# First image of two chained attention layers: the half blocks from the sixth on are loaded in 128-byte runs and turned by VectorE

## The chip, the cores and the metric

One core of a Trainium2 chip runs the whole program. The metric is the device time of one execution in microseconds (us), the median of the runs. A core has five engines that work at the same time and wait for one another by semaphores: TensorE (PE, and PEld for its weight loads), VectorE (DVE), ScalarE (ACT), GpSimd (POOL) and SyncE (SP). Each takes its own instructions in the order in which they stand in the program. SP and POOL here mostly start DMA transfers.

## What is computed

Two self-attention layers over four images of 64x64 pixels with 256 channels, that is 4096 tokens of 256 float32 values per image:

```python
# layer 0, per image: x is (4096, 256)
q, k, v = x @ Wq + bq, x @ Wk + bk, x @ Wv + bv        # 32, 32 and 256 wide
x = gamma * (softmax(q @ k.T) @ v) + x
# layer 1
g, f, v = x @ Wg + bg, x @ Wf + bf, x @ Wh + bh        # 32, 32 and 128 wide
x = x + (softmax(g @ f.T) @ v) @ Wo + bo
```

## The kernel before

The kernel goes through image `b`, layer `l`, block of queries `j` and, innermost, step `i` over groups of keys. In layer 0 a block has 256 queries and a step takes 512 keys, so there are eight steps. `Step.scores` makes the scores `st` (L532) and their exponentials `high` and `p` (L542, L544); `cut_low` and `cut_both` split the rounding off into `low` and `d` (L555, L560); `products_first` multiplies the parts with the parts of v (L580).

Before an image can be attended to, its tokens have to be projected. This is done by half blocks of 256 tokens, `h` from 0 to 15 (`NH`), and `project_units(b, l, h)` returns three pieces of work:

- `transpose_unit` makes `xT`, the tokens turned so that channels lie on the partitions, and its two parts `xh` (L405, ScalarE) and `xl` (L406, VectorE), in the list `x_parts`.
- `qk_unit` makes the projections q and k in the bank `psqk` (L422), collects them in `qk` and splits them into `qk_parts` (L439 to L442), writes these to DRAM (`qk_dram`, L446, on SP) and, in the first image, loads k straight from them by four transfers on POOL (`load_k`, L493).
- `v_unit` makes v in the bank `psv` (L464) and its three parts `v0h`, `v0l`, `v0d` (L480 to L483).

There are two ways to turn a half block. For image 0, layer 0, the tokens are loaded as they lie (`load_first`, tiles `x_nat`, L300), turned by TensorE into a PSUM bank `psx` (L389) and copied out by ScalarE (L390). `LEAD` = 5 halves are loaded at the start; from then on the transpose of half h starts the load of half h+5. In all other cases `load_squares` fetches a half with eight transfers of 32 channels each (L280), whose runs are 32 values, 128 bytes, in such a way that squares of 32x32 values lie where VectorE's transpose of such squares (L392) turns them into `xT`.

The banks `psx`, `psqk` and `psv` come from a pool of two, `ps_side`. In SBUF, image 0 also uses buffers that layer 1 needs only later: the tag `v1` (10 buffers, `V1`) holds `x_nat`, and the tag `v1_parts` (6 buffers, `LEAD_BUFS`) holds `xT`, both parts and `qk_parts` of the odd halves. The even halves have buffers of their own (`xT`, `squares`, `qk_parts`).

The first six halves of image 0 are projected ahead of all steps (L685 to L689). The other ten go two by two into the first five steps: at the head of step i the transposes of halves 2(i+3) and 2(i+3)+1 are written (`early`, L761 to L763), and their `qk_unit` and `v_unit` follow behind part of the products (L789 to L790). Later images are projected during layer 1 of the image before.

The text gives the order in which work is named; a scheduler then sets the order in which the instructions of each engine stand, from its own estimate of when the inputs are there. That order is fixed when the kernel runs.

## Time and profile before

| | |
|---|---|
| three runs | 3155.88 us median, 3155.57 to 3157.44 |
| the profiled execution | 3156.87 us, its span 3155.1 us |
| busy: PE, DVE, ACT, POOL | 3117.6, 2689.3, 2138.5, 898.7 us |
| granted TensorE clock | 0.998 of full speed |
| projection of image 0, layer 0 (first to last `xT` copy of L390) | from 5.6 to 79.0 us |
| L389 transposes on TensorE | 64 instructions, 0.299 us each |
| L390 copies on ScalarE | 16, 0.584 us each |
| `x_nat` loads on SP | 32 of 128 KB |

The profile is of one execution. Its times are microseconds from the start of the span; TensorE's ends are modelled, and its matmuls overlap, so a busy TensorE isn't one at its peak. A line of a timeline gives the start, the busy time, engine, line and operation, the tiles written and read with their shapes, and in brackets for how long the engine had been idle before, and what ended that.

### The profile page before, as it was taken

Reading aid. Unit: us, or ns where it says so; the run is one execution under the profiler, and the core shown is the slowest. Engines: PE = TensorE matmul, PEld = TensorE weight load, DVE = VectorE, ACT = ScalarE, POOL = GpSimd, SP = SyncE. Lnnn points to the kernel's source line nnn. Section 1 sums busy time; section 2 is a strip of 40 time slices with the busy share of each in tenths; the row PEclk is TensorE's granted clock in tenths of the full one; section 3 lists DMA queues with packets and bytes.
Section 4 is the critical chain, followed back from the end, with each engine's and each line's share of the span. In section 5 each row is a group of like instructions: output and inputs, shape, how many; then the busy total and the mean of one; then the engine's idle time right before and its main releaser. Section 6 shows DMA issues by size and latency. Waiting matters only on the chain.

```text
span 3155.1 us, 54090 instructions
## 1 busy us (share of the span) xinstructions
PE 3117.6 (99%) x19908; PEld 2674.3 (85%) x19908; DVE 2689.3 (85%) x3237; ACT 2138.5 (68%) x2835; POOL 898.7 (28%) x1108
## 2 busy tenths in 40 slices
PE   8999999999999999999999999999999999999997
PEld 7999998666799999866689999976668999996664
DVE  7888888888888888988888888888888888888876
ACT  7666666777666666777766666677776666666664
POOL 5222224222422222422242222332223222233221
PEclk9999999999999999999999999999999999999999
DMA  4121114555512121455541112255554111125454
GB/s 122 40 53 47 47 49 104 108 105 107 102 43 51 43 51 47 113 101 112 107 94 45 50 44 53 51 117 105 106 113 80 48 46 46 49 66 105 97 96 73
DMA packets 391392, 239.49 MB, mean 76 GB/s; under 512 B 266672, under 2 KB 355248, under 8 KB 391120
## 3 DMA queue, kind: packets, MB, share of 16 engines
q0 software_dynamic: 68160, 134.86, 22.0%
q1 hardware_dynamic: 322048, 100.76, 13.3%
q8 instruction: 161, 2.64, 0.4%
q14 instruction: 111, 0.91, 0.1%
q10 hardware_dynamic: 912, 0.33, 0.0%
HBM read 82.58 MB, written 67.11 MB: 47 GB/s over the span
## 4 chain that ended last, share of the span: by engine, by line
PE 91%; DVE 3%; issue 2%; DMA 2%; ACT 1%; POOL 0%; SPq 0%; DVEq 0%; ACTq 0%; POOLq 0%
PE acc L580 23%; PE acc_pair L580 23%; PE acc L598 23%; PE st L532 14%; PE psv L464 4%; PE psqk L422 2%; PE pso L665 2%; DVE low L555 1%; DMA squares<-in_x 1%; DVE d L560 1%; ACT p L544 1%; DVE p_sum L573 1%; DMA p_sum_moved<-p 0%; PE pso L666 0%; DMA squares<-x_dram 0%
## 5 line engine op out<-in xcount | busy, mean ns | idle before, releaser
L542 ACT ACTIVATE high<-st,down 128x1024 fp32r<-128x1024 f32 x704 | 785.8, 1116 | 707.2 <-PE st L532 419.5
L544 ACT ACTIVATE p<-st 128x1024 f32<-128x1024 f32 x1024 | 1042.2, 1021 | 167.5 <-PE st L532 145.8
L560 DVE SCALAR_TENSOR_TENSOR d<-low,high 128x1024 fp32r<-128x1024 f32 x704 | 870.5, 1237 | 227.7 <-PE acc_pair L580 222.3
L555 DVE TENSOR_TENSOR low<-p,high 128x1024 fp32r<-128x1024 f32 x704 | 938.5, 1333 | 142.7 <-ACT p L544 141.7
L532 PE MATMUL st<-q,k 128*128 128x256 f32 (+1 forms) x3072 | 703.7, 337 | 2.8 <-issue 1.3
L598 PE MATMUL acc<-p,v 128*128 128x512 f32 x1280 | 611.0, 597 | 0.0
L532 PEld LDWEIGHTS st<-q,k 128*128 128x128 f32 x3072 | 470.7, 189 | 102.9 <-issue 41.3
L637 POOL TENSOR_TENSOR x_res<-x,bo 128x256 f32<-128x256 f32 x128 | 213.9, 1671 | 879.5 <-DVE x L626 879.4
L598 PEld LDWEIGHTS acc<-p,v 128*128 128x128 f32 x1280 | 233.2, 189 | 161.8 <-issue 143.4
L573 DVE TENSOR_TENSOR p_sum<-p_sum,p 128x1024 f32<-128x1024 f32 x288 | 352.6, 1224 | 10.4 <-ACT p L544 6.8
L580 PE MATMUL acc<-v0h,high 128*128 128x258 f32 x2048 | 342.4, 284 | 1.2 <-ACT high L542 1.2
L580 PE MATMUL acc<-v0d,d 128*128 128x258 f32 x2048 | 339.3, 287 | 2.4 <-DVE d L560 2.0
L580 PE MATMUL acc<-v0l,low 128*128 128x258 f32 x2048 | 331.5, 283 | 0.6 <-DVE low L555 0.5
L580 PE MATMUL acc_pair<-v0l,low 128*128 128x258 f32 x2048 | 331.1, 283 | 0.0
L580 PE MATMUL acc_pair<-v0h,high 128*128 128x258 f32 x2048 | 329.6, 283 | 0.0
L580 PE MATMUL acc_pair<-v0d,d 128*128 128x258 f32 x2048 | 329.0, 283 | 0.0
L580 PEld LDWEIGHTS acc<-v0h,high 128*128 128x128 f32 x2048 | 287.2, 189 | 3.1 <-issue 1.4
L580 PEld LDWEIGHTS acc<-v0d,d 128*128 128x128 f32 x2048 | 280.9, 189 | 5.4 <-DVE d L560 4.7
L580 PEld LDWEIGHTS acc<-v0l,low 128*128 128x128 f32 x2048 | 281.7, 190 | 1.8 <-DVE low L555 1.3
L580 PEld LDWEIGHTS acc_pair<-v0h,high 128*128 128x128 f32 x2048 | 282.4, 189 | 0.0
L580 PEld LDWEIGHTS acc_pair<-v0l,low 128*128 128x128 f32 x2048 | 281.8, 189 | 0.0
L580 PEld LDWEIGHTS acc_pair<-v0d,d 128*128 128x128 f32 x2048 | 281.8, 189 | 0.0
(108 smaller groups left out, 3326.6 us busy)
## 6 DMA issues: line engine op xcount, KB each, us to landing
p_sum_moved<-p POOLq DMA_DIRECT2D x160, 512.0 KB, 4.8
x_res<-in_x SPq DMA_DIRECT2D x128, 128.0 KB, 2.1
qk_dram<-qk_parts SPq DMA_DIRECT2D x128, 128.0 KB, 1.8
x_dram<-x SPq DMA_DIRECT2D x128, 128.0 KB, 1.7
out<-x_res SPq DMA_DIRECT2D x128, 128.0 KB, 1.7
squares<-x_dram SPq DMA_DIRECT2D x512, 32.0 KB, 2.0
out<-y POOLq DMA_DIRECT2D x128, 128.0 KB, 3.2
q<-qk_dram POOLq DMA_DIRECT2D x252, 64.0 KB, 2.2
```

The source lines that it names most:

```text
L422: nc.tensor.matmul(ps, wqk[l][:, c, :], x_parts[key][n][:, c, :], start=(c == n == 0), stop=(c == NCC - 1 and n == 1),)
L464: nc.tensor.matmul(ps[:, t, :], xT[key][:, c, t * P : (t + 1) * P], wv[l][:, c, :], start=(c == 0), stop=(c == NCC - 1),)
L532: nc.tensor.matmul(st[:, g, :], k_t[b, l, kt // NT][:, kt % NT * P : (kt % NT + 1) * P], q_t[b, l, j * n // QB][:, q0 : q0 + n], start=Tru ...
L542: nc.scalar.activation(self.high, s_flat, AF.Exp, bias=down)
L544: nc.scalar.activation(self.p, s_flat, AF.Exp)
L555: nc.vector.tensor_sub(self.low, self.p, self.high.bitcast(F32))
L560: nc.vector.scalar_tensor_tensor(self.d, self.low.bitcast(F32), -UP, self.high.bitcast(F32), ALU.mult, ALU.add)
L573: nc.vector.tensor_add(p_sum, p_sum, self.p)
L580: nc.tensor.matmul(acc[2 * s + which][:, :W], p[:, g * QB0 + s * P : g * QB0 + (s + 1) * P], v0[self.i][v][:, g, :], start=self.first and ...
L598: nc.tensor.matmul(acc[which], v_part[:, g, :], p[:, g * QB : (g + 1) * QB], start=first and g == 0, stop=last and g == G[1] - 1,)
L637: nc.gpsimd.tensor_add(x_old[s], x_new[s], bo_sb)
L665: nc.tensor.matmul(ps[:, :C], part, wo_sb, start=True, stop=True)
```

## The change

From half 5 on, image 0 takes the second way too. `load_first` stops after the first five halves. The transpose of half h, from h = 3 on, starts the load of half h+2 with `load_squares`, into buffers of the tag `v1_parts`; and for h of 5 and above `transpose_unit` takes the branch with VectorE's transpose. Nothing else is edited: the split into parts, the projections and the attention are as they were, and so are the later images.

```diff
+    LEAD_BUFS = sum(split[1])
 
     def load_squares(key, tokens):
 
-        t = work.tile([P, NCC, QB0], F32, tag="squares", bufs=2, name="squares_" + "_".join(map(str, key)))
+        first = key[:2] == (0, 0)
+        t = (data if first else work).tile(
+            [P, NCC, QB0],
+            F32,
+            tag="v1_parts" if first else "squares",
+            bufs=LEAD_BUFS if first else 2,
+            name="squares_" + "_".join(map(str, key)),
+        )
         for c in range(NCC):
             for a in range(P // S):
                 ch = c * P + a * S
...
-    LEAD_BUFS = sum(split[1])
     LEAD = V1 // NS
 
     def load_first(h):
-        if h < NH:
+        if h < LEAD:
             x_nat[h] = []
...
-            if b == l == 0:
+            if b == l == 0 and h < LEAD:
                 ps = side_psum(f"psx_{h}").rearrange("p (c n) -> p c n", c=NCC)
...
             nc.scalar.copy(x_parts[key][0], xT[key])
             nc.vector.tensor_sub(x_parts[key][1], xT[key], x_parts[key][0].bitcast(F32))
-            if b == l == 0:
-                load_first(h + LEAD)
+            if b == l == 0 and h + 2 >= LEAD:
+                load_half(b, h + 2)
```

## The prediction

> **What bounds the kernel now.** I read the page first (engine totals, then the chain that ended last), then busy time by stretches over the first 100 us, then VectorE's and ScalarE's timelines there, then the line of the VectorE transposes.

> ```profile
> PE 3117.6 (99%) x19908; PEld 2674.3 (85%) x19908; DVE 2689.3 (85%) x3237; ACT 2138.5 (68%) x2835; POOL 898.7 (28%) x1108
> ...
> PE 91%; DVE 3%; issue 2%; DMA 2%; ACT 1%; POOL 0%; SPq 0%; DVEq 0%; ACTq 0%; POOLq 0%
> ```

> Over the span TensorE sets the time. But the change acts only while the first image is projected, so only that stretch may be asked. Five stretches, one for each step that projects two half blocks:

> ```profile
> 34.45:45.90 11.45, 11.42 (x76) 10.27 (x75) 9.53 (x14) 9.50 (x21) 4.96 (x11) 1.00 0.42 105
> 45.90:56.97 11.07, 9.70 (x61) 8.17 (x58) 8.56 (x15) 7.89 (x16) 5.06 (x11) 1.00 0.40 101
> 56.97:65.91 8.94, 8.16 (x51) 7.21 (x52) 6.27 (x11) 6.71 (x13) 2.69 (x6) 1.00 0.33 83
> 65.91:75.82 9.91, 9.56 (x61) 8.43 (x60) 7.83 (x13) 7.99 (x17) 3.88 (x8) 1.00 0.24 55
> 75.82:85.56 9.74, 9.37 (x62) 8.31 (x60) 7.72 (x12) 7.83 (x17) 3.88 (x8) 1.00 0.24 55
> ```

> After the length come PE, PEld, DVE, ACT and POOL. TensorE is nearly full here too, but VectorE and ScalarE work 8 of 10 us each, so this stage is a relay among three engines. VectorE's part of one step:

> ```profile
> 75.70 1.23 DVE L555 TENSOR_TENSOR low<-p,high 128x1024 fp32r<-128x1024 f32 x1 [0.77 <-ACT p L544]
> 76.95 0.42 DVE L442 TENSOR_TENSOR qk_parts<-qk,qk_parts 64x256 fp32r<-64x256 f32 x1
> 77.40 1.23 DVE L560 SCALAR_TENSOR_TENSOR d<-low,high 128x1024 fp32r<-128x1024 f32 x1
> 78.55 0.68 DVE L482 SCALAR_TENSOR_TENSOR v0d<-v0h,psv 128x512 fp32r<-128x512 f32 x1
> 79.14 0.68 DVE L406 TENSOR_TENSOR xl<-xT,xh 128x512 fp32r<-128x512 f32 x1
> 79.75 0.68 DVE L483 SCALAR_TENSOR_TENSOR v0l<-v0d,v0h 128x512 fp32r<-128x512 f32 x1
> 80.35 0.68 DVE L406 TENSOR_TENSOR xl<-xT,xh 128x512 fp32r<-128x512 f32 x1
> ```

> The two `xl` stand 1.2 us apart: the next two halves are turned and split early, side by side, while the last half's `v0d`, `v0l` and the step's `d` fill VectorE. The pitch is that of `psv` of the odd halves, 64.07, 73.99, 83.91: 9.92 us.

> ```profile
> L392 DVE STREAM_TRANSPOSE xT<-squares x112: 685/704/715, 113.6 to 2864.8; 128x512 f32<-128x512 f32 x112
> ```

> ```profile
> squares<-in_x SPq DMA_DIRECT2D x384, 32.0 KB, 2.5
> x_nat<-in_x SPq DMA_DIRECT2D x32, 128.0 KB, 3.0
> ```

> So the new operations have prices here, from the later images: 0.704 us for a transpose, 2.5 us to land.

> [...] `v0d` at 78.55 was ready at 77.19, when the reading of the accumulator ended, and waited behind `d`. [...] 1.25 us from `low` (75.70) to `qk_parts`, which writes partitions 64 to 127, but 1.15 from `d` (77.40) to `v0d`. [...]

> **The change, part by part.** Halves 5 to 15 change.

> Removed: 44 TensorE transposes (four advance the chain of waits by 0.44 us: 4.8 us), 11 ScalarE copies (0.586 each, 6.4 us), 22 loads on SP (0.41 each by 37.03, 9 us).

> Added: 11 VectorE transposes (7.7 us) and 88 loads on SP. Their issue has a median of 0.45 us: 40 us. Per step SP issues 16x0.45+2x0.34 = 7.9 us, which fits either pitch.

> Buffers: the allocator's placement puts even halves' `squares` where an `xl`, `xT` or `xh` had been, and odd ones from 11 on where the previous odd `squares` stood. That load waits for its transpose. SP in one step: after the last `qk_dram` eight loads for half h+2, eight for h+3, then `qk_dram` of h and h+1. The second eight start at 7.2 us into the step (below), take 3.6 to issue (5.1 at the worst group's 5.08 for eight) and 2.5 to land, so are there by 15; their transpose comes at 20. `qk_dram` of h is up to 3 us later than it could be; its buffer is next written about 7 us after that has landed. Hidden. The transpose in turn waits for its eight loads, and all of VectorE's queue stands behind it, ScalarE's `xh` too; by these times that wait is over before the queue gets there.

> What isn't hidden is the order. In the built program the VectorE order of one steady step (h even) is: T(h), xl(h), qk(h), v0d(h), v0l(h), T(h+1), low, xl(h+1), qk_parts(h), d, qk(h+1), v0d(h+1), v0l(h+1), qk_parts(h+1), T(h+2). T is the transpose. Each T stands behind the whole projection of the half before it, so the halves run one after the other. I walk through it with rows of before, T(h) starting at 0.

> Even half. T ends at 0.70; `xh` on ScalarE (0.62) ends at 1.35; TensorE starts `psqk` at 1.40 and, in the same order as before, `v0h` starts 2.60 later (79.07 to 81.67): 4.00. `v0d` starts 1.21 after `v0h` when nothing lies between (21.52 to 22.73): 5.21. `v0l` 0.72 later (22.73 to 23.45), T(h+1) 0.61 after that: **6.54**.

> Odd half. ScalarE comes to `high` at 5.2, `p` at 6.2 (1.01, 83.56 to 84.57), `low` 1.05 later (74.65 to 75.70): 7.27. ScalarE then does `qk_parts` (7.1) and `xh` (7.45 to 8.07). VectorE: `xl` 8.41, `qk_parts` 9.12, `d` 9.57, `qk` 10.72. TensorE from 8.1: `v0h` at 10.7, so `v0d` 11.9, `v0l` 12.6, `qk_parts` held until 13.3, next T at **13.8**.

> So the pitch is 13.8 instead of 9.92, although VectorE has only 1.3 us more to do. TensorE's saving falls in its own waits: it stands about 2 us for each `xh`.

> Sum. Orders hardly differ up to `v0d` of half 5, 36.32 before. T(6) follows it: 0.6 later, and 0.3 for T(5) in front of it (VectorE had gaps for the rest), 37.2. Four pitches to T(14): 55.2. Once VectorE's `bo` addition stands between (56.49 before): 0.35. In the last step `qk_parts` of half 15 stands before `v0l` and ends at 13.05. Together 105.8; before it ended at 86.87+0.42 = 87.3. From there both walk the same path (k loads, the step's scores 2.57 us after, `high`): the order from there on is the same on all five engines. **+18.5 us**. The profiled execution took 3156.87 around its span of 3155.1; its sum is 3175.4. On the median of 3155.88 that is **3174.4 us**.

> Unknown: the k loads beside the 128-byte loads. They land 2.2 us after issue, at 2.6 into the step, and are needed at 4.2; above 2 us more each further us costs up to 5. Below, they can gain nothing, as nothing waits for them. I take 0. The walk's hand-overs may be off by 0.5 us a step either way: 2.5. TensorE waits longer, but showed a granted clock of 1.00 with 2.70 busy of 4 us between 12 and 20.

> **Rivals.** *The lighter TensorE wins.* The chain of waits holds 0.44+0.65 us of `psx` per step. Without them, and with psx out of the two side banks, 9.92 becomes 8.8; VectorE's 7.8+1.3 = 9.1 binds: 5x0.8 = 4 us less, 3152. For it: TensorE is the fullest engine. Against: it needs both T ahead of the previous half's end, and the order does not have that. It decides if T(h+1) starts within about 2 us of T(h). This one is not slower.

> *SP binds.* Above (13.8-0.7)/16 = 0.82 us per issue SP is later than the relay. At 1.0 the pitch is 16.7: 14 us more, 3189. For it: single issues reach 2.0 us, in-order waits. Against: the median of 0.45 over 384.

> *Half of it.* If ScalarE and TensorE take up the odd half earlier than the walk says, say 2 us a step, it is +8.5: 3164.

> **How the numbers follow.** Forecast 0.78 (own range 3170 to 3180), half 0.10, SP 0.07, lighter TensorE 0.05. The range 3168.5 to 3181.5 is the forecast's with the walk's error (2.5), late k loads above (up to one us in each of the five steps), the first step's start (1) and a little towards the other cases; half, SP and lighter TensorE are left out, 0.22 together, of which a part of the half reaches in. 0.2% is 6.3 us, about what a measurement of this kernel can tell from no change. Slower by more than that: 0.78+0.07 and 0.09 of the half, 0.94; within: 0.01 of the half and 0.04 of the lighter TensorE, 0.05; faster: 0.01.

> **What would show it.** VectorE's transposes of halves 6, 8, 10, 12, 14 some 13.8 us apart, and each odd one 6.5 after its even one; no wait of VectorE for a `squares` DMA in the first 110 us; TensorE busy well below 9 of 10 in these steps; the same pitch as before from step 8 on, all of it 18 us later. Wrong: transposes in pairs, or waits for `squares`.

## The result, and the profile after

The changed kernel takes 3186.8 us, the median of five runs (3184.64 to 3187.75), beside 3156.29 for the kernel before. The ratio is 1.0091, 95% interval 1.008 to 1.0102: 30.5 us slower on the medians (28.7 by the ratio), where 18.5 were forecast and 3181.5 was the upper end of the range. The profiled execution took 3184.64 us, its span 3182.9 us, 27.8 more than the span of before.

The page of the kernel after, its row of granted clocks over the span, and the chain's shares by engine:

```profile
PEclk9899999999999999999999999999999999999999
...
PE 92%; DVE 2%; issue 2%; DMA 1%; ACT 1%; SPq 1%; POOL 0%; DVEq 0%; ACTq 0%; POOLq 0%
```

The shares say as little as they did before. The row of clocks has one slice that isn't at 9: the second, 80 to 160 us. The stretches from one even half's transpose to the next (the last one ends with `qk_parts` of half 15), with length, PE, PEld, DVE, ACT, POOL, granted clock, DMA share and GB/s:

```profile
37.80:52.98 15.18, 11.39 (x62) 9.77 (x60) 11.04 (x17) 6.82 (x14) 5.21 (x12) 0.89 0.45 87
52.98:67.85 14.87, 10.41 (x54) 8.98 (x54) 9.75 (x16) 6.71 (x14) 4.03 (x9) 0.89 0.37 72
67.85:84.34 16.49, 11.63 (x52) 9.87 (x52) 9.60 (x14) 6.79 (x14) 3.91 (x8) 0.79 0.33 64
84.34:100.78 16.44, 12.21 (x52) 10.55 (x52) 9.51 (x14) 6.71 (x14) 3.91 (x8) 0.69 0.34 65
100.78:114.69 13.91, 10.01 (x52) 8.62 (x52) 8.82 (x13) 6.71 (x14) 3.53 (x8) 0.88 0.15 36
```

A step is 15 to 16.5 us long instead of about 10. TensorE is busy for only 7 of 10 us in it, although for more microseconds than before (11.6 in the third stretch, 9.6 in the last but one of before) and without the 44 transposes: its matmuls got slower, as the granted clock, the last column but two, says. VectorE in the second of these steps, halves 8 and 9:

```profile
52.98 0.70 DVE L399 STREAM_TRANSPOSE xT<-squares 128x512 f32<-128x512 f32 x1
54.37 0.69 DVE L413 TENSOR_TENSOR xl<-xT,xh 128x512 fp32r<-128x512 f32 x1 [0.68 <-ACT xh L412]
56.49 0.48 DVE L447 SCALAR_TENSOR_TENSOR qk<-psqk,bqk,qk 64x256 f32<-64x256 f32 x1 [1.42 <-ACT qk L446]
58.10 0.69 DVE L489 SCALAR_TENSOR_TENSOR v0d<-v0h,psv 128x512 fp32r<-128x512 f32 x1 [1.14 <-ACT v0l L488]
58.83 0.69 DVE L490 SCALAR_TENSOR_TENSOR v0l<-v0d,v0h 128x512 fp32r<-128x512 f32 x1
59.44 0.70 DVE L399 STREAM_TRANSPOSE xT<-squares 128x512 f32<-128x512 f32 x1
```

This is the walk of the prediction row by row: the transpose of half 9 starts 6.46 us after that of half 8 (6.54 were worked out), directly behind `v0l`, and not because of its data: nothing stands in brackets behind it. In the whole stage VectorE shows no wait for a `squares` DMA. SP is the one that waits: 12.2 us in four waits between 28 and 116 us, for VectorE's transposes to free its buffers. In the second step the `qk_dram` of half 8 stood behind them: its `qk_parts` were done at 62.31, but it was issued at 64.07, after the sixteen loads from 52.97 to 63.96.

What the walk doesn't have is seen on TensorE, in the fourth stretch:

```profile
85.76 0.38 PE L429 MATMUL psqk<-xh,wqk 128*128 128x256 f32 x1 [2.39 <-ACT xh L412]
85.98 1.02 PE L471 MATMUL psv<-wv,xT 128*128 128x256 f32 x4
...
87.19 1.85 PE L471 MATMUL psv<-wv,xT 128*128 128x256 f32 x4
88.48 0.99 PE L539 MATMUL st<-q,k 128*128 128x256 f32 x2
91.31 1.23 PE L587 MATMUL acc<-v0h,high 128*128 128x258 f32 x4 [1.84 <-ACT high L549]
...
93.42 1.91 PE L471 MATMUL psv<-wv,xT 128*128 128x256 f32 x4
```

Four matmuls for `psv` take 1.02 us, then, 1.2 us later, the same four take 1.85, and 1.91 at 93.42. TensorE had waited 2.39 us for `xh` shortly before; when it waits 1.84 us for `high`, it is already slow. The same stretch in the columns of above, cut at the times at which the granted clock can be seen to change:

```profile
83.83:87.24 3.41, 1.48 (x9) 1.38 (x10) 1.85 (x4) 0.62 (x1) 1.11 (x3) 1.00 0.49 104
87.24:90.66 3.42, 2.23 (x7) 1.58 (x6) 0.85 (x2) 1.95 (x5) 0.00 (x0) 0.50 0.32 50
90.66:94.07 3.41, 2.76 (x11) 2.67 (x12) 3.34 (x6) 2.32 (x4) 0.98 (x2) 0.50 0.10 17
94.07:97.48 3.41, 3.41 (x11) 2.79 (x11) 2.12 (x3) 0.37 (x1) 0.98 (x2) 0.50 0.54 94
97.48:100.90 3.42, 2.33 (x19) 2.13 (x17) 1.92 (x4) 1.46 (x4) 0.98 (x2) 1.00 0.23 58
```

A stretch in which TensorE was busy for only 1.48 of 3.41 us is followed by three at half clock.

Four explanations had to be told apart. Theory A: the serial order costs the 18 us of the walk, and the clock that TensorE loses in the waits of that order costs the rest. Rival B: the 88 loads in 128-byte runs bind through SP or their landing. Rival C: VectorE's eleven transposes cost more than their 7.7 us show. Rival D: the order alone has all of it, and the low clock only goes along with the waits.

### The profile page after: what moved, and what is told of

Its sections match the earlier page's. It is cut to its first block, busy times and chain, and to the rows that moved or that the text cites. A ratio compares the mean times of both kernels' runs of the same rounds, so it can differ in the third digit from the quotient of the medians.

```text
span 3182.9 us, 54104 instructions
## 1 busy us (share of the span) xinstructions
PE 3125.9 (98%) x19864; PEld 2681.5 (84%) x19864; DVE 2693.9 (85%) x3248; ACT 2131.7 (67%) x2824; POOL 901.3 (28%) x1108
## 3 DMA queue, kind: packets, MB, share of 16 engines
q1 hardware_dynamic: 342816, 100.76, 13.5%
## 4 chain that ended last, share of the span: by engine, by line
PE 92%; DVE 2%; issue 2%; DMA 1%; ACT 1%; SPq 1%; POOL 0%; DVEq 0%; ACTq 0%; POOLq 0%
PE acc L605 24%; PE acc L587 23%; PE acc_pair L587 23%; PE st L539 14%; PE psv L471 4%; PE psqk L429 2%; PE pso L672 2%; SPq L288 1%; ACT p L551 1%; DMA p_sum_moved<-p 0%; PE pso L673 0%; DMA squares<-in_x 0%; DVE d L567 0%; DVE low L562 0%; DMA squares<-x_dram 0%
## 5 line engine op out<-in xcount | busy, mean ns | idle before, releaser
L587 PE MATMUL acc<-v0h,high 128*128 128x258 f32 x2048 | 343.3, 285 | 10.2 <-ACT high L549 10.2
L587 PEld LDWEIGHTS acc<-v0h,high 128*128 128x128 f32 x2048 | 287.8, 190 | 13.1 <-ACT high L549 11.6
## 6 DMA issues: line engine op xcount, KB each, us to landing
x_res<-in_x SPq DMA_DIRECT2D x128, 128.0 KB, 2.1
qk_dram<-qk_parts SPq DMA_DIRECT2D x128, 128.0 KB, 1.8
x_dram<-x SPq DMA_DIRECT2D x128, 128.0 KB, 1.7
out<-x_res SPq DMA_DIRECT2D x128, 128.0 KB, 1.7
out<-y POOLq DMA_DIRECT2D x128, 128.0 KB, 3.2
```

Of the source, the lines that this page charges most:

```text
L587: nc.tensor.matmul(acc[2 * s + which][:, :W], p[:, g * QB0 + s * P : g * QB0 + (s + 1) * P], v0[self.i][v][:, g, :], start=self.first and ...
```

## The experiments

All times are beside the kernel before on the same chip, whose median was 3158.57, 3159.08 and 3159.88 us in the three sessions; the ratios take that out. Line numbers move by a few from kernel to kernel.

**late: the serial order alone.** The kernel before, with one piece of work named later:

```diff
-            run([u[0] for u in early])
+            run([early[0][0]])
...
-                run(early[0][1:] + early[1][1:])
+                run(early[0][1:] + early[1])
```

> The kernel before, with one thing changed: the transpose of each odd half from 7 on is named behind the v projection of the even half before it. TensorE still transposes, nothing is loaded in 128-byte runs, VectorE has no transposes; but on VectorE xl of the odd half now stands behind v0l of the even half, as in the changed kernel. Theory A (the halves run one after the other because VectorE's queue holds the next half's work behind the last half's v parts, and TensorE, waiting about 2 us for each xh, then loses its clock): most of the 28 us comes back without any of the new loads: 3176 to 3188, pitch of the even halves 13.5 to 16, granted clock at 0.5 to 0.8 in stretches between 45 and 115 us. Rival B (the 128-byte loads on SP and their landing cost it) and rival C (the eleven VectorE transposes cost it): 3154 to 3160, clock 1.00.

Measured: 3175.62 us, ratio 1.0047 (1.003 to 1.0064). Three of its steps, from one even half's `xl` to the next, in the same columns as above:

```profile
39.86:51.62 11.76, 10.27 (x68) 9.03 (x68) 8.12 (x13) 7.79 (x16) 3.19 (x7) 1.00 0.25 63
51.62:65.91 14.29, 11.30 (x62) 9.54 (x60) 8.54 (x15) 7.80 (x16) 4.59 (x10) 0.88 0.31 83
65.91:77.51 11.60, 9.30 (x60) 8.40 (x61) 8.21 (x13) 7.69 (x16) 3.73 (x8) 1.00 0.20 54
```

With none of the new loads and none of the new transposes half of the loss is there, so B and C can't be the whole. It is a little less than theory A gave (3176 to 3188): the pitch is 11.3 to 11.8 us where the clock stays at 1.00, not 13.5. Here only `xl` stands in VectorE's queue behind `v0l`; the transpose itself is on TensorE and its copy on ScalarE, so those two links aren't in the chain. The 14.29 us step is one in which the clock fell.

**pairs: VectorE's order alone put right.** The changed kernel, with `qk` and `v0d` of each even half held behind the odd half's transpose:

```diff
+    def behind_turn(b, l, h):
+        own = b == l == 0 and h > LEAD and h % 2 == 0
+        return tc.issue_after(turns[b, l, h + 1].ins) if own else nullcontext()
...
+            with behind_turn(b, l, h):
+                nc.vector.scalar_tensor_tensor(whole, ps[top, :], bqk[l], whole, ALU.add, ALU.add)
```

> The changed kernel with one order forced: qk and v0d of each even half from 6 on stand behind the transpose of the odd half after it on VectorE. Same transposes, same loads, still two halves ahead. Theory A: the two halves of a step overlap again, pitch 10 to 12.5, TensorE fuller and its clock mostly 1.00, 3160 to 3170; what is left over 3156 would be the queue's head (the next even half still stands behind v0l of the odd one) or a wait for squares that now shows, since the odd half's loads have less time. Rival B (loads): the loads are the bound, so 3182 or more, with VectorE waiting for squares. Rival C (VectorE's extra work): at most 5 us better than the changed kernel, 3180 or more.

Measured: 3186.24 us, ratio 1.0085 (1.0068 to 1.0102): nothing gained, a miss for theory A as it was put. The time is what B and C had said; but VectorE shows no wait for `squares` here either, and C is tested by the run early below. ScalarE's timeline shows why nothing was gained:

```profile
54.73 0.37 ACT L451 COPY qk<-psqk 64x256 f32<-64x256 f32 x1 [1.75 <-PE psqk L434]
55.54 0.60 ACT L493 ACTIVATE v0h<-psv 128x512 fp32r<-128x512 f32 x1 [0.44 <-PE psv L477]
56.03 0.59 ACT L494 ACTIVATE v0l<-psv 128x512 fp32r<-128x512 f32 x1
56.51 0.20 ACT L494 ACTIVATION_READ_ACCUMULATOR v0l<-psv 128x1 f32 x1
56.60 1.12 ACT L556 ACTIVATE high<-st,down 128x1024 fp32r<-128x1024 f32 x1
57.60 1.04 ACT L558 ACTIVATE p<-st 128x1024 f32<-128x1024 f32 x1
58.50 0.64 ACT L417 CAST xh<-xT 128x512 fp32r<-128x512 f32 x1
```

The odd half was turned at 53.63 to 54.33, but its `xh` stands on ScalarE behind the even half's `qk`, `v0h` and `v0l` and the step's `high` and `p`, until 58.50. So the serial order lies in more than one engine's queue; freeing VectorE's moved the wait to ScalarE's.

**deep: loads further ahead.** The new loads go into the buffers that held `x_nat`, so that they run five halves ahead, and the scheduler is left to find its own order:

```diff
-            if b == l == 0 and h + 2 >= LEAD:
-                load_half(b, h + 2)
+            if b == l == 0:
+                load_half(b, h + LEAD)
```

> The changed kernel, but the halves in 128-byte runs go into two tiles each of the tag that held x_nat, so that they are loaded five halves ahead as before, and VectorE's transpose is two of 128x256 for a half. The order that comes out has the transposes of the next two halves ahead of the last half's v0d and v0l. The number of bytes, DMAs and transposed elements is that of the changed kernel. Theory A: pitch 9.1 to 10.5 (VectorE has 7.8+1.4 us of work in a step), clock 1.00, 3150 to 3162. Rival B (the 88 loads on SP bind, 0.45 to 0.5 us each, 7.2 to 8 a step): no better than the pitch they allow, and since they queue further ahead, SP in front of qk_dram: 3175 or more. Rival C (eleven transposes' worth of VectorE work): 3180 or more.

Measured: 3168.11 us, ratio 1.0028 (1.0018 to 1.0038). Two thirds of the loss go, with every load and every transposed element still there. Against the pitch of 9.1 to 10.5 it is a miss: a step is 13.1 us long (the transposes of halves 9 and 11 start at 54.41 and 67.52), shorter than in the changed kernel, but in an order that is again not that of before. For rivals B and C, which have no reason to expect a gain here, it is a miss as well.

**pinned2 and pinned: the old order with the new work.** On VectorE, ScalarE and TensorE the order of the kernel before is written out as a table, from the projection of half 4 to that of half 15, without the TensorE transposes and their copies, and with each pair of VectorE transposes ahead of `v0d` of the half before. pinned2 has the changed kernel's own loads, pinned those of deep:

```diff
+    for name, order in ORDER.items():
+        own = [i for i in nc.cur_bb.bb.instructions if i.engine == getattr(mybir.EngineType, name)]
+        for a, b in zip(order, order[1:]):
+            tc.add_manual_dep(
+                own[b],
+                own[a].name,
...
```

> The same pinned order, but with the changed kernel's own loads and buffers, two halves ahead. The sixteen loads for the next pair start when the two transposes free their buffers, take 16 x 0.45 = 7.2 us to issue and 2.5 to land, so the next pair is there 9.7 us or a little more after this one. Theory A: 3150 to 3165, with waits of VectorE for squares of up to 2 us a step that the slower order had hidden. Rival B: 3176 or more with long waits for squares. Rival C: 3166 or more without such waits.

> The loads of the run deep (128-byte runs, five halves ahead), VectorE's transposes, and on VectorE, ScalarE and TensorE exactly the order of the kernel before, from the projection of half 4 to that of half 15; only the TensorE transposes and the copies of them are gone, and VectorE's transposes of halves h and h+1 stand ahead of v0d of half h-1. Theory A (only the order costs): the halves overlap as before, VectorE with 9.1 to 9.3 us of work in a step is about as full as TensorE, pitch 9.1 to 10.2, clock 1.00: 3148 to 3160. Rival B (88 loads in 128-byte runs bind, or disturb the k loads) or rival C (the eleven transposes of VectorE cost their 0.7 us each and more): 3166 or more.

Measured: pinned2 3164.61 us, ratio 1.0016 (1.0009 to 1.0024); pinned 3166.63 us, ratio 1.0024 (1.0013 to 1.0034). pinned2 lies in the range put down for theory A; pinned doesn't (3148 to 3160), it lies just inside that of B and C, a miss for A. In pinned2 nothing is changed in the kernel but the order, and about four fifths of the loss are gone (0.0091 to 0.0016). That settles B as the cause of it: the same 88 loads, the same two halves of lead, and over the whole stage VectorE waits once for `squares`, 0.57 us. What is left shows on VectorE and ScalarE of pinned2:

```profile
73.01 1.23 DVE L567 SCALAR_TENSOR_TENSOR d<-low,high 128x1024 fp32r<-128x1024 f32 x1
74.15 1.30 DVE L399 STREAM_TRANSPOSE xT<-squares 128x512 f32<-128x512 f32 x2
75.37 0.65 DVE L489 SCALAR_TENSOR_TENSOR v0d<-v0h,psv 128x512 fp32r<-128x512 f32 x1
...
74.89 1.21 ACT L412 CAST xh<-xT 128x512 fp32r<-128x512 f32 x2 [2.09 <-DVE xT L399]
```

The two transposes stand behind `low`, `qk_parts` and `d`, and ScalarE waits for them (2.09 us here) before it can make `xh`. In the kernel before TensorE turns its halves while it works on the products, so that wait doesn't exist. Part of what is left is the clock: it falls in two steps of pinned2 as well, to 0.88 and 0.86 on the mean.

**early: and the transposes ahead of `low`.** As pinned, with the last three pairs of transposes one place earlier.

> The run pinned, with the transposes of the pairs 10 and 11, 12 and 13, 14 and 15 one place further ahead on VectorE, in front of low of the step before instead of v0d: in pinned ScalarE still waited 1.3 to 2.1 us a step for them, a wait the kernel before hasn't, since TensorE turns its halves while the products run. Theory A: three steps lose that wait, 4 to 6 us less than pinned, a ratio to the kernel before of 0.999 to 1.001. Rival C (VectorE's added work itself is what pinned still pays): no change against pinned, 1.0024, since VectorE's work is the same.

Measured: 3162.49 us, ratio 1.0008 (1.0 to 1.0017). The gain against pinned is 4.1 us on the medians of two sessions and 5.1 by the ratios, as theory A had it. So rival C falls too as the cause of the loss: all of VectorE's transposes, and all 88 loads, are in this kernel, and it is at most 0.17% from the kernel before. That is up to 5 us; what of it the added work costs isn't told apart. Two of its steps:

```profile
58.55:69.58 11.03, 9.14 (x56) 7.88 (x55) 9.39 (x19) 6.72 (x15) 3.88 (x9) 1.00 0.52 105
69.58:79.94 10.36, 8.81 (x54) 7.63 (x53) 9.06 (x17) 6.72 (x15) 3.87 (x9) 1.00 0.23 52
```

VectorE works 9.1 to 9.4 us of a step of 10.4 to 11, now a little more than TensorE. No version ran that beats the kernel before.

**warm and warm4: the clock alone.** The changed kernel with its own order held by such a table, and matmuls added that only keep TensorE busy; their result is overwritten by the projection that follows in the same bank:

```diff
         def qk_unit():
             ps = side_psum(f"psqk_{b}_{l}_{h}")[:, :QB0]
+            for n in range(12 if b == l == 0 and h > LEAD else 0):
+                nc.tensor.matmul(ps, wqk[0][:, 0, :], v0[0]["h"][:, 0, :QB0], start=True, stop=True)
```

> The changed kernel with its order on VectorE, ScalarE and TensorE pinned as it is, and in each half from 6 on twelve matmuls of 128x256 more on TensorE, whose result is overwritten: for the even half ahead of psqk, for the odd half ahead of the products with high, the two places where TensorE waits for about 2 us. Each is 0.11 us at full clock, so they take 1.3 us of the wait. Theory A with the clock as its second part: TensorE no longer loses its clock, the pitch is the 13.8 of the walk, and the time is 3170 to 3179, faster than the changed kernel although it has 120 matmuls more. Rival D (the lower clock is only a companion of the waits and costs nothing, the serial order has all of the 28 us): 3184 to 3192 with the clock at 1.00.

> The run warm with four extra matmuls in place of twelve at each of the two waits: 0.44 us, so that waits of about 2.0 to 2.3 us become 1.6 to 1.9. If the clock falls only when one wait is longer than some length near 2 us: clock 1.00 and the time of warm, a ratio of 1.005 to 1.006. If it falls with the idle share of several us, the clock falls in part of the steps: 1.006 to 1.0085. If even 0.44 us do nothing: 1.009, and the twelve helped for another reason than the clock.

> The changed kernel itself, beside the other two on one chip: a ratio to the kernel before of 1.008 to 1.010. It is here so that what the extra matmuls give is read against it and not only against the kernel before.

Measured: warm 3177.03 us, ratio 1.0056 (1.0042 to 1.0069); warm4 3179.45 us, ratio 1.0063 (1.005 to 1.0077); the changed kernel again, in the session of warm4, 3185.61 us, ratio 1.0082 (1.0068 to 1.0096). The steps of warm:

```profile
39.71:53.26 13.55, 12.43 (x87) 11.41 (x86) 10.96 (x18) 6.83 (x14) 5.61 (x13) 1.00 0.52 97
53.26:67.02 13.76, 12.89 (x87) 11.36 (x86) 9.66 (x17) 6.72 (x14) 3.62 (x8) 1.00 0.41 78
67.02:80.70 13.68, 11.67 (x77) 10.18 (x76) 9.51 (x14) 6.80 (x14) 3.90 (x8) 1.00 0.41 78
80.70:94.27 13.57, 12.15 (x80) 10.64 (x80) 9.44 (x14) 6.71 (x14) 3.92 (x8) 1.00 0.40 77
94.27:107.07 12.80, 11.00 (x71) 9.47 (x69) 8.73 (x13) 6.71 (x14) 3.54 (x8) 1.00 0.17 40
```

A kernel with 120 matmuls more is faster: by the ratios, 0.0026 to 0.0035 of 3159, 8 to 11 us for warm; for warm4, beside the changed kernel on one chip, 6.2. VectorE and ScalarE do the same work in the same order, TensorE too but for the added matmuls; what differs is the clock, which is 1.00 from 39.71 to 107.07. Rival D is out. The pitch is 13.55 to 13.76, where the walk had 13.8. warm4 came out as the second of its three cases: between 45 and 110 us the clock fell in one step alone (0.83 on the mean from 55 to 65 us; four matmuls for `psv` took 1.03 us at 54.80 and 1.91 at 61.40). Its waits between 39 and 61 us were no longer than 1.37, so here it fell without a wait of about 2 us.

From the transpose of half 6 to the start of `qk_parts` of half 15 the changed kernel takes 114.27 - 37.80 = 76.5 us, warm 106.65 - 39.71 = 66.9, warm4 108.11 - 39.63 = 68.5. So up to there 8 to 9.5 us of the loss are the clock, 8 being a lower bound, since warm4 still lost some; the serial order has the other 18. End to end warm can gain less than that, because in its profile half 5 was turned 2 us later than in the changed kernel, before the added matmuls begin (the last section has that).

## Why the prediction was right in kind and wrong in size

Right, by its own steps:

- What isn't hidden is the order. The built order of a step was read before the run, and the trace shows it instruction for instruction. T(6) was put at 37.2 and stands at 37.80. Even halves were 6.54 long; those with the clock at 1.00 measure 6.63, 6.46 and 6.47.
- SP and the loads were costed at nothing, because the relay covers them: shown by pinned2 and by the one wait of 0.57 us that appears only when the relay is faster. That the runs are 128 bytes long shows in no time either: early has all 88 loads and is within 0.17% of the kernel before.
- VectorE's added 7.7 us were not what made the kernel slower: early has them too. The removed work of TensorE gained nothing, as said.
- The walk's pitch of 13.8: shown by warm, 13.55 to 13.76.
- From the end of `qk_parts` of half 15 on both kernels take the same path, and the k loads cost nothing: the scores follow 2.67 us later (2.57 before). The clock isn't the same, though. In the changed kernel TensorE has run out of work and stands 2.88 us until k is there, where the kernel before still had products to do; its clock is then 0.50 from 117.96 to 124.79, and the difference grows from 27.4 to 29.0 us within two steps. That it is 27.8 at the end is chance: it drifts between 27.5 and 31.2 on the way.

Wrong, one step: "TensorE waits longer, but showed a granted clock of 1.00 with 2.70 busy of 4 us between 12 and 20." With it the prediction put the cost of the clock at nothing. The end of `qk_parts` of half 15 was put at 105.8 and came at 114.69, 8.9 us later. The terms: 0.6 from T(6); 62.98 us from T(6) to T(14) instead of 55.2 + 0.35, so 7.4; 13.91 instead of 13.05 for the last step, 0.9. All the odd halves and two of the five even ones ran with a clock of 0.68 to 0.80 on the mean; the four pitches with the clock held are 13.55 + 13.76 + 13.68 + 13.57 = 54.6.

The term was in the text and was read from the wrong stretch: between 12 and 20 us TensorE is idle for a third of the time, but in waits of at most 1.30 us. The walk itself said that TensorE would stand about 2 us for each `xh`. The profile of before has waits of that length only at its start (3.20 us) and at its end (4.79 us up to 3144.02, where the clock is 0.50), none in the stretch that was read. So the walk had no row for such a wait, and the clock was taken at its better end. For the other end it had what was needed: 2.60 us of each half, from `psqk` to `v0h`, is TensorE on the chain. At half clock in all ten halves that is 26 us more, an estimate from that row. The range left this end out and had only 2.5 us for hand-overs; 8.9 came of it.

Of the rivals, SP binds is refuted (pinned2). The lighter TensorE wins is refuted as well, and more strictly than was argued: even with T(h+1) directly behind T(h), which the text named as the point from which it decides, pinned, pinned2 and early aren't faster than before. In early VectorE, busy for 9.1 to 9.4 us of a step of 10.4 to 11.0, is fuller than TensorE; that this is why TensorE's saved work gains nothing is argued, not tested.

The size of the fall is in the changed kernel's own trace: the granted clock is 0.50 from 87.24 to 97.48 us, and the four matmuls for `psv` take 1.85 and 1.91 us there, instead of 1.02. Its clock changes only at edges that lie 3.41 us, or a multiple of that, apart. No long wait was needed for it: no wait of TensorE between 36 and 115 us is longer than 2.39 us.

How empty such a window of 3.41 us was can be read from the profiles of before and after (the last section has the counts): of those at full clock each with less than 1.5 us of TensorE's work in it was followed by half clock, and none with 2.11 us or more. Between 12 and 20 us of before TensorE has 2.1 us and more in each window. A wait of 2 us that lies in one window leaves at most 1.4. In warm no stretch of 3.41 us between 40 and 107 us has less than 2.3.

What stays open: why of the three windows between 1.5 and 2.1 us one was followed by half clock (1.69 us) and two not (1.78 and 2.09). TensorE's ends are modelled, which may be part of it. That wasn't tried further.

## What to carry to other kernels

When a tile starts to arrive another way, a scheduler that works from estimates may order everything behind it anew; read the new order on each engine before counting what the new instructions cost, because a relay of three engines can lose more to a late place in a queue, here 18 us, than to 7.7 us of added work. When such an order makes TensorE wait longer than anywhere in the profile at hand, price its matmuls at half clock as well as at full, and count how much work is left in the emptiest stretches: in the profiles of before and after a clock of 0.50 followed each window of 3.41 us, from 12 us on, with less than 1.5 us of it. To tell an order from the work in it, hold the order fixed and change the work, or the other way round; freeing one engine's queue alone showed nothing here.

## What the runs showed of the hardware

Twelve matmuls whose result nobody reads, 1.56 to 1.67 us of busy time in each wait of about 2, made the kernel 8 to 11 us faster; four of them, 0.63 to 0.73 us, had most of that effect (3179.45 against 3185.61 us).

The clock can also differ where the program doesn't. Up to half 6 warm4 has the loads of the changed kernel and its order on VectorE, ScalarE and TensorE, but between 20 and 24 us its granted clock was 0.57, where the changed kernel had 1.00 in both of its profiles; half 5 was then turned at 31.35 us instead of 28.66 and 29.52. It began before the clock fell: ScalarE waited 1.85 us for VectorE's `qk` (0.79 in the changed kernel), the next `xT` was copied at 18.98 us instead of 18.02, and TensorE was busy for 2.00 us between 16 and 20 us instead of 2.70. What held VectorE up isn't shown. VectorE was 1.0 us late at the next `xl` (21.40 instead of 20.43) and 1.8 us at the `v0d` behind it (25.00 instead of 23.17). Such a dip before the stage in question moves everything after it, so stages are better compared from one of their own events than from the start of the span.
